# Four summing groups instead of five in layer 0's attention, and a transposed block end in layer 3

## Chip, cores and metric

The kernel runs on one core of a Trainium2 chip. The metric is device time in microseconds (us) from launch to end; lower is better. The core has five engines with queues of their own: TensorE (PE in the profile, with its weight loads as PEld) multiplies matrices into PSUM, VectorE (DVE) and ScalarE (ACT) work elementwise, GpSimd (POOL) does small things here, and SyncE (SP) issues the transfers between HBM and SBUF.

## What is computed

Four layers run one after the other on x of shape (2, 128, 64, 64), each as x = x + layer(group_norm(x)). The change touches the attention of the first and of the last. Cut to these:

```python
# layer 0, per head (4 heads, 32 channels each, n = m = 4096 pixels)
attn1 = softmax(einsum('bhnc,bhmc->bhnm', q1, k1) * temperature, axis=-1)
out1 = einsum('bhnm,bhmc->bhnc', attn1, v)
...
out = conv1x1(out1 + out2, w_po)
...
# layer 3, per head (8 heads, 16 channels each)
a = softmax(einsum('bhcq,bhck->bhqk', q, k) / sqrt(C), axis=-1)
o = einsum('bhqk,bhck->bhcq', a, v)
return o.reshape(B, C, h, w)
```

`out2` is a small attention over channels in layer 0; layers 1 and 2 are convolutions and a product in the Fourier domain. They are left as they are.

## The kernel before

**Softmax in both layers.** No maximum is subtracted (a bound on the exponents is checked at the end, and a general version would run if it were passed). The kernel computes exp(scores), multiplies these weights with the values, and divides the result by the sum of the weights over the keys.

**Layer 0's attention** (`attention` inside `_layer0`, with `_attn_four`). It runs once for each of the two batches. The queries are cut into 8 blocks (`qb`) of 512, the keys into 32 tiles (`kt`) of 128. For each tile of keys, TensorE computes the scores of four heads into two PSUM tiles `ps_s` (L1343; three such tiles exist), ScalarE turns each into `weights` (L1352, 128x1024 each; both halves are one buffer, of which there are four), and TensorE multiplies `vt` with these weights into the accumulator `ps_acc0` (L1760, called by `multiply` one tile behind the scores). PSUM holds the accumulator until the block's last tile; then ScalarE copies it to `used` (L1790).

The sum of the weights takes a second path. VectorE adds the weights of several key tiles elementwise (L1800: `sums`, 128x2048 each, two buffers). How many tiles form such a group says `SUMMED`, by default five groups of 7, 6, 7, 6 and 6 tiles. A group of n tiles takes n - 1 additions: the first tile is only held. When a group is complete, it is put in `pending`, and at the fourth tile of the next group TensorE multiplies it with a block of ones (L1760 again, `sums` and `ones`), which sums over the 128 keys of a tile and accumulates over the groups in `ps_acc1`. After the last group of a block, VectorE transposes that PSUM tile in blocks of 32x32 (`by_query`, L1773), takes the reciprocal of one column in 32 (`rec`, L1775), transposes it back, spread over 32 rows, into `q1` (L1776), and multiplies `used` with it (L1780). `by_query` shares one buffer with the tile `g` of the normalization.

Beside the attention of batch 0 run, woven in one step at every fourth key tile, the channel attention of batch 0 and the normalization of batch 1 (`normalize`: ScalarE makes `g`, TensorE transposes it, VectorE computes statistics and scales, TensorE transposes back). Beside the attention of batch 1 run its channel attention and the statistics of batch 0. Unlike most of the kernel, `attention` isn't inside `_in_order`: the order of its instructions on an engine is that of the tile framework's scheduler. What follows it is in order: batch 1's convolutions after batch 0, and `finish`, the output projection, after batch 1.

**Layer 3's attention** (`attend` inside `_layer3`) is inside `_in_order`. It runs four times (two batches, two halves `t` of the heads), each over 8 blocks of 512 queries and 32 key tiles. Per key tile TensorE computes scores (L2102), ScalarE exponentials (L2112, 128x1024, two per tile), and TensorE multiplies the values two tiles behind (L2121). Here the sums come with the product: the stationary operand holds 16 columns of values and 16 columns of ones for each head, so that in each 32 rows of the accumulator 16 rows are the output and 16 rows the sums, the latter repeated 16 times; which half is which alternates from head to head. There are two accumulators in PSUM; the running block holds one, and the side work that makes the next queries, keys and values uses the other in turn.

At a block's end `done` (L2131) loads the residual of the 64 rows by four DMAs from X, copies the accumulator out of PSUM to `u`, exchanges the halves of each 32 rows into `r` by a stream shuffle, takes the reciprocal of all of `r` (128x512), multiplies, adds the residual, and stores the rows that matter by four DMAs. The 32 block ends are spread over the stage; the last one is the end of the program.

Of the kernel before, what the change touches and what calls it, by code (L numbers as in the profile page):

```python
# [10 lines left out]
F32 = mybir.dt.float32  # L11
# [7 lines left out]
CH = 512  # L19
# [1265 lines left out]


LIMIT = 60.0
SUMMED = (7, 6, 7, 6, 6)
F32R = mybir.dt.float32r
ENGINES = (  # L1290
    mybir.EngineType.PE,
# [117 lines left out]
def _layer0(ctx, tc, X, a, cst, worst, there, dram):  # L1409
# [10 lines left out]
    def acc(n):  # L1420
        return accp.tile([128, CH], F32, tag=f"acc{n}", name=f"ps_acc{n}")
# [330 lines left out]
    def attention(pool, side):  # L1752
        ac = [None, None]
        parts, pending, used = [None], [], {}
        places = [(n, i) for n, size in enumerate(SUMMED) for i in range(size)]

        def four(n, lhs, w, first, last):
            for j in range(4):
                rows = slice(32 * j, 32 * j + 32)
                nc.tensor.matmul(ac[n][rows, :], lhs(rows), w[:, j, :], start=first, stop=last)  # L1760

        def sums():

            while pending:
                qb, n, w = pending.pop(0)
                if n == 0:
                    ac[1] = acc(1)
                four(1, lambda rows: ones, w, n == 0, n == len(SUMMED) - 1)
                if n == len(SUMMED) - 1:

# [11 lines left out]
        def multiply(qb, kt, w):  # L1782
# [13 lines left out]
            else:  # L1796
# [7 lines left out]
                )  # L1804
            if i == SUMMED[n] - 1:
                pending.append((qb, n, parts[0]))
# [156 lines left out]
def _layer3(ctx, tc, X, l3, cst, out, worst, here):  # L1963
    nc = tc.nc
# [4 lines left out]
    two = ctx.enter_context(tc.tile_pool(name="f3_two", bufs=2))  # L1969
# [4 lines left out]
    def acc():  # L1974
        return accp.tile([128, CH], F32, tag="acc", name="ps_acc")
# [118 lines left out]
    def attend(b, t, q, k, vt, early):  # L2094
        ac = [None]

        def scores(qb, kt):
            ps = [spp.tile([128, 2, CH], F32, tag="sp", name="ps_s") for _ in range(2)]
            for n in range(2):
                for j in range(4):  # L2100
                    rows = slice(32 * j, 32 * j + 32)
                    nc.tensor.matmul(  # L2102
                        ps[j // 2][:, j % 2, :],
                        k[rows, kt * 128 : (kt + 1) * 128],
                        q[n][rows, qb * CH : (qb + 1) * CH],
                        start=(n == 0),
                        stop=(n == 1),
                    )
            w = []
            for p in range(2):  # L2110
                w.append(pp.tile([128, 2, CH], F32, tag="weights", name="weights"))
                nc.scalar.activation(w[p], ps[p], AF.Exp)  # L2112
            return w

        def multiply(qb, kt, w):
            if kt == 0:
                ac[0] = acc()
            for j in range(4):

                i = j % 2  # L2120
                nc.tensor.matmul(  # L2121
                    ac[0][32 * j : 32 * j + 32, :],
                    vt[:, kt, j // 2, i : i + 2, :].rearrange("p a d -> p (a d)"),
                    w[j // 2][:, i, :],
                    start=(kt == 0),
                    stop=(kt == NQT - 1),
                )
            if kt == NQT - 1:
                done(qb, ac[0])

        def done(qb, ps):  # L2131
            cols = slice(qb * CH, (qb + 1) * CH)

            places = [
                (slice(32 * j + 16 * (j % 2), 32 * j + 16 * (j % 2) + 16),
                 slice(64 * t + 16 * j, 64 * t + 16 * j + 16))
                for j in range(4)
            ]
            xs = residual[qb % 2]
            for to, rows in places:  # L2140
                nc.sync.dma_start(xs[to, :], X[rows, b, cols])
            u = two.tile([128, CH], F32, tag="u", name="u", bufs=1)
            nc.vector.tensor_copy(u, ps)  # L2143
            r = two.tile([128, CH], F32, tag="r", name="r", bufs=1)
            nc.vector.stream_shuffle(r, u, [(i + 16) % 32 for i in range(32)])  # L2145
            nc.vector.reciprocal(r, r)  # L2146
            nc.vector.tensor_mul(u, u, r)  # L2147
            nc.vector.tensor_add(u, u, xs)  # L2148
            for at, rows in places:
                nc.sync.dma_start(out[b, rows, cols], u[at, :])  # L2150

        waiting = []
        for qb in range(NCH):
            for kt in range(NQT):
                if kt % 2 == 0:
                    over = next(early, early) is early
                waiting.append((qb, kt, scores(qb, kt)))
                if len(waiting) > 2:
                    multiply(*waiting.pop(0))
                yield kt if over else None  # L2160
        for x in waiting:
            multiply(*x)
# [187 lines left out]
```

## Time and profile before

| What | us |
|---|---|
| median of 3 runs | 4205.69 |
| lowest and highest run | 4199.02, 4210.75 |
| the profiled execution's own time | 4197.72 |
| its span, first to last instruction | 4195.9 |
| PE busy | 4026.9 |
| ACT busy | 3332.9 |
| DVE busy | 2127.8 |
| POOL busy | 71.3 |

The profile is of one execution, and its own time stands beside the runs' median: it is one of the shorter ones. Busy shares are means over stages with different limits, so the numbers that matter are those of a stage or of one block, read in the timeline and in windows. Layer 0's two attentions run from about 193 to 806 us and from 1003 to 1596 us, layer 3 from about 2200 us to the end. A line such as `sums<-sums,weights` gives the tile written, then the tiles read; the numbers behind the bar are the busy time of a group in us and the mean of one in ns, and after the second bar stands the idle time ahead of it and what ended it. In the records each fp32 matmul counts twice, so eight records of L1760 are one step of four matmuls.

### The profile page before, as it was taken

The numbers are of one execution on the slowest core, as the hardware profiler recorded it, in microseconds if no ns is written. First come the engines' busy times: TensorE is split into PE (matmuls) and PEld (weight loads), VectorE is DVE, ScalarE is ACT, GpSimd is POOL, SyncE is SP. The second block draws the span as 40 slices with busy tenths as digits, with TensorE's granted clock in tenths as the row PEclk, the third lists the DMA queues.
The fourth block names the chain that finished last, engine by engine and source line by source line (L and its number), as shares of the span: only waits on it lengthen the run. The fifth ranks groups of instructions, "written<-read, shape, count | busy, mean of one in ns | idle before, by whom it ended". The sixth has DMA issues, their size and how long they took to land. (4 is left out here: it accounts for less than half of the span.)

```text
span 4195.9 us, 90633 instructions
## 1 busy us (share of the span) xinstructions
PE 4026.9 (96%) x40014; PEld 1494.0 (36%) x40014; DVE 2127.8 (51%) x2374; ACT 3332.9 (79%) x4035; POOL 71.3 (2%) x145
## 2 busy tenths in 40 slices
PE   7999999989999998997999999999999999999998
PEld 4522222354222224445664333333333333333332
DVE  4678888657888888986754112221132102211111
ACT  4478888735888883326647999999999999999998
POOL 1001000010000001000000000000000000000000
PEclk9999999999999999998999999999999999999999
DMA  1199960000000000004750000000000000000000
GB/s 49 29 188 182 179 90 1 2 2 2 2 1 2 2 1 12 1 1 171 290 208 4 6 6 6 4 6 6 4 6 6 6 4 6 6 4 6 6 6 5
DMA packets 158855, 159.40 MB, mean 38 GB/s; under 512 B 24809, under 2 KB 148713, under 8 KB 154354
## 3 DMA queue, kind: packets, MB, share of 16 engines
q1 hardware_dynamic: 158450, 153.50, 15.7%
q8 instruction: 315, 5.16, 0.5%
q14 instruction: 90, 0.74, 0.1%
HBM read 145.09 MB, written 73.40 MB: 52 GB/s over the span
## 5 line engine op out<-in xcount | busy, mean ns | idle before, releaser
L2112 ACT ACTIVATE weights<-ps_s 128x1024 f32<-128x1024 f32 x2048 | 1884.8, 1099 | 62.8 <-PE ps_s L2102 62.3
L1352 ACT ACTIVATE weights<-ps_s 128x1024 f32<-128x1024 f32 x1024 | 992.9, 1023 | 180.6 <-PE ps_s L1343 164.2
L2121 PE MATMUL ps_acc<-weights,vt 128*32 128x512 f32 x8192 | 1092.8, 605 | 0.0
L2102 PE MATMUL ps_s<-q,k 32*128 32x512 f32 x8192 | 924.9, 444 | 5.4 <-ACT weights L2112 5.4
L1800 DVE TENSOR_TENSOR sums<-sums,weights 128x2048 f32<-128x2048 f32 x352 | 806.7, 2292 | 38.4 <-ACT weights L1352 5.2
L2102 PEld LDWEIGHTS ps_s<-q,k 32*128 32x128 f32 x8192 | 471.2, 182 | 839.4 <-ACT weights L2112 773.6
L1343 PE MATMUL ps_s<-q,k 32*64 32x512 f32 x8192 | 627.3, 613 | 7.1 <-ACT weights L1352 2.4
L1760 PE MATMUL ps_acc<-weights,vt 128*32 128x512 f32 x4096 | 550.9, 606 | 6.6 <-ACT weights L1352 3.6
L2143 DVE COPY u<-ps_acc 128x512 f32<-128x512 f32 x32 | 22.1, 691 | 1039.0 <-PE ps_acc L2121 1039.0
L1343 PEld LDWEIGHTS ps_s<-q,k 32*64 32x64 f32 x8192 | 159.6, 130 | 436.4 <-PE ps_s L1343 320.3
L2121 PEld LDWEIGHTS ps_acc<-weights,vt 128*32 128x32 f32 x8192 | 162.9, 108 | 379.2 <-issue 367.2
L1800 DVE TENSOR_TENSOR sums<-weights 128x2048 f32<-128x2048 f32 x80 | 183.3, 2291 | 113.6 <-ACT weights L1352 113.6
L1760 PEld LDWEIGHTS ps_acc<-weights,vt 128*32 128x32 f32 x4096 | 81.2, 108 | 426.3 <-issue 403.3
L662 DVE SCALAR_TENSOR_TENSOR X<-g,w,X 128x2048 f32<-128x2048 f32 x84 | 197.4, 2350 | 2.6
L1548 PE MATMUL ps_sp<-pad,diag 32*32 32x512 f32 x4608 | 158.9, 597 | 2.3 <-ACT q L1568 1.3
L1008 PE MATMUL ps_z<-w_ri,e 128*32 128x128 f32 x2048 | 137.3, 408 | 14.3 <-DVE e L950 12.1
L2063 DVE TENSOR_TENSOR vt<-ps_acc,bv 128x384 f32<-128x384 f32 x32 | 17.8, 557 | 246.0 <-PE ps_acc L2056 246.0
L1548 PEld LDWEIGHTS ps_sp<-pad,diag 32*32 32x32 f32 x4608 | 95.0, 103 | 54.2 <-issue 15.9
L2033 DVE LOAD_MASK_SELECT qq<-ps_acc x32 | 0.4, 14 | 222.6 <-PE ps_acc L2030 222.6
L2146 DVE RECIPROCAL r<-r 128x512 f32<-128x512 f32 x32 | 107.3, 3353 | 1.1
L950 DVE TENSOR_SCALAR e<-ps_pe 32x136 f32<-32x136 f32 (+1 forms) x352 | 104.4, 297 | 4.9
L948 ACT ACTIVATE e<-ps_pe 32x136 f32<-32x136 f32 (+1 forms) x352 | 99.2, 282 | 4.1
(289 smaller groups left out, 2552.5 us busy)
## 6 DMA issues: line engine op xcount, KB each, us to landing
w_ri<-w_r SPq DMA_DIRECT2D x16, 2112.0 KB, 8.2
w_ri<-w_i SPq DMA_DIRECT2D x16, 2112.0 KB, 13.5
w_r<-in_L_conv_kr_w SPq DMA_DIRECT2D x15, 528.0 KB, 13.5
w_r<-in_L_conv_kr_x SPq DMA_DIRECT2D x15, 528.0 KB, 13.3
w_r<-in_L_conv_kr_y SPq DMA_DIRECT2D x15, 528.0 KB, 13.0
w_r<-in_L_conv_kr_z SPq DMA_DIRECT2D x15, 528.0 KB, 13.2
w_i<-in_L_conv_ki_w SPq DMA_DIRECT2D x15, 528.0 KB, 13.8
w_i<-in_L_conv_ki_x SPq DMA_DIRECT2D x15, 528.0 KB, 12.7
```

The lines of the kernel that those rows point to most:

```text
L662: nc.vector.scalar_tensor_tensor(xi, g[:, i : i + H // 2, j : j + W], w8[:, s : s + 1], xi, ALU.mult, ALU.add)
L950: nc.vector.tensor_scalar_mul(out, got[of, :, s], sign)
L1008: nc.tensor.matmul(out.rearrange("p (n f o) -> p n f o", n=2, f=2), e[:, s, 2 * j : 2 * j + 2, :].rearrange("p f x -> p (f x)"), w.rearran ...
L1343: nc.tensor.matmul(ps[j // 2][to, j % 2, :], k[rows, kt * 128 + 64 * half : kt * 128 + 64 * half + 64], q[rows, qb * CH : (qb + 1) * CH], ...
L1352: nc.scalar.activation(w[:, 2 * p : 2 * p + 2, :], ps[p], AF.Exp)
L1548: nc.tensor.matmul(ps[r // 2][to, r % 2, :].rearrange("p (h w) -> p h w", w=W), diag[rows, grp, t, :], pad[rows, y0 : y0 + ROWS, t % 3 : t ...
L1760: nc.tensor.matmul(ac[n][rows, :], lhs(rows), w[:, j, :], start=first, stop=last)
L1800: nc.vector.tensor_add(parts[0].rearrange("p j c -> p (j c)"), t.rearrange("p j c -> p (j c)"), w.rearrange("p j c -> p (j c)"),)
L2102: nc.tensor.matmul(ps[j // 2][:, j % 2, :], k[rows, kt * 128 : (kt + 1) * 128], q[n][rows, qb * CH : (qb + 1) * CH], start=(n == 0), stop= ...
L2112: nc.scalar.activation(w[p], ps[p], AF.Exp)
L2121: nc.tensor.matmul(ac[0][32 * j : 32 * j + 32, :], vt[:, kt, j // 2, i : i + 2, :].rearrange("p a d -> p (a d)"), w[j // 2][:, i, :], star ...
L2146: nc.vector.reciprocal(r, r)
```

## The change

Two edits. In layer 0 the 32 key tiles of a block form four groups of eight in place of five groups of six or seven: 28 additions on VectorE per block where there were 27, and four matmul groups with `ones` where there were five. In layer 3 the block end is written another way: the accumulator is transposed in blocks of 32x32 straight from PSUM into `z`, so that a query's 16 sums lie along the free axis; the reciprocal is then taken of one column per block of 32, 16 columns in all, for each of the four groups of 32 partitions on its own, since the column alternates; a multiplication with these spread over 32 columns follows, a second transpose brings the result back into `u`, and the addition of the residual and the DMAs stay as they were. The copy, the stream shuffle and the reciprocal over 512 columns are gone. The tile `r` becomes 16 columns wide, with two buffers instead of one, and `z` is new, of 512 columns with one buffer.

```diff
-SUMMED = (7, 6, 7, 6, 6)
+SUMMED = (8, 8, 8, 8)
...
             for to, rows in places:
                 nc.sync.dma_start(xs[to, :], X[rows, b, cols])
+            z = two.tile([128, CH // 32, 32], F32, tag="z", name="z", bufs=1)
+            flat = z.rearrange("p n i -> p (n i)")
+            nc.vector.transpose(flat, ps)
+            r = two.tile([128, CH // 32], F32, tag="r", name="r")
+            for j in range(4):
+                rows = slice(32 * j, 32 * j + 32)
+                nc.vector.reciprocal(r[rows, :], z[rows, :, 16 * (1 - j % 2)])
+            nc.vector.tensor_mul(z, z, r.unsqueeze(2).to_broadcast([128, CH // 32, 32]))
             u = two.tile([128, CH], F32, tag="u", name="u", bufs=1)
-            nc.vector.tensor_copy(u, ps)
-            r = two.tile([128, CH], F32, tag="r", name="r", bufs=1)
-            nc.vector.stream_shuffle(r, u, [(i + 16) % 32 for i in range(32)])
-            nc.vector.reciprocal(r, r)
-            nc.vector.tensor_mul(u, u, r)
+            nc.vector.transpose(u, flat)
             nc.vector.tensor_add(u, u, xs)
             for at, rows in places:
                 nc.sync.dma_start(out[b, rows, cols], u[at, :])
```

## The prediction

> **What bounds the kernel now.** I read the page first, its busy table and its 40 slices, to see which engine fills which stage.
>
> ```profile
> PE   7999999989999998997999999999999999999998
> DVE  4678888657888888986754112221132102211111
> ACT  4478888735888883326647999999999999999998
> ```
>
> Two stages are touched. Layer 0's attention lies in slices 2 to 8 and 10 to 16 (195 to 806 us and 1003 to 1596 us): TensorE is full and VectorE is close behind. Layer 3 is the right half: TensorE and ScalarE are full, VectorE nearly empty. Next, the costliest groups:
>
> ```profile
> L2112 ACT ACTIVATE weights<-ps_s 128x1024 f32<-128x1024 f32 x2048 | 1884.8, 1099 | 62.8 <-PE ps_s L2102 62.3
> ...
> L1800 DVE TENSOR_TENSOR sums<-sums,weights 128x2048 f32<-128x2048 f32 x352 | 806.7, 2292 | 38.4 <-ACT weights L1352 5.2
> L2102 PE MATMUL ps_s<-q,k 32*128 32x512 f32 x8192 | 924.9, 444 | 5.4 <-ACT weights L2112 5.4
> ...
> L2146 DVE RECIPROCAL r<-r 128x512 f32<-128x512 f32 x32 | 107.3, 3353 | 1.1
> ```
>
> L1800 is the addition that layer 0 does once per key tile, except at a group's first: 352 + 80 = 432 = 16 blocks x 27. L2146 is the reciprocal that the change shrinks: large, but on an engine on which layer 3 does not wait. The PE rows of layer 3 lost only 5.4 us waiting.
>
> What matters is one layer 0 block. The window view over a block without side work (from one `used` copy to the next) and over the block with batch 1's normalization beside it:
>
> ```profile
> 588.15:660.64 72.49, 72.24 (x816) 16.15 (x808) 64.00 (x32) 62.47 (x67) 0.00 (x0) 1.00 0.15 18
> 273.54:368.10 94.56, 89.03 (x886) 23.73 (x894) 77.82 (x109) 76.18 (x89) 15.23 (x8) 0.96 1.03 186
> ```
>
> Columns after the stretch: length, then busy PE, PE weight loads, DVE, ACT, POOL. The clean block is TensorE's: 72.24 of 72.49 us. VectorE has 8.5 us over, ScalarE 10. The other block is 22 us longer and nobody is full in it.
>
> The timeline of PE shows the price of one summing matmul group (`ones`), whose starts I subtract:
>
> ```profile
> 652.56 1.28 PE L1343 MATMUL ps_s<-q,k 32*64 32x512 f32 x16
> 653.77 1.07 PE L1760 MATMUL ps_acc<-weights,vt 128*32 128x512 f32 x8
> 654.65 1.04 PE L1760 MATMUL ps_acc<-sums,ones 128*32 128x512 f32 x8
> 655.62 1.11 PE L1343 MATMUL ps_s<-q,k 32*64 32x512 f32 x16
> ...
> 668.46 1.04 PE L1760 MATMUL ps_acc<-sums,ones 128*32 128x512 f32 x8
> ...
> 684.15 1.04 PE L1760 MATMUL ps_acc<-sums,ones 128*32 128x512 f32 x8
> ...
> 697.80 1.04 PE L1760 MATMUL ps_acc<-sums,ones 128*32 128x512 f32 x8
> ```
>
> The timeline of VectorE around the same block end shows its slack:
>
> ```profile
> 672.51 0.71 DVE L1773 STREAM_TRANSPOSE by_query<-ps_acc 128x512 f32<-128x512 f32 x1
> ...
> 679.49 2.28 DVE L1800 TENSOR_TENSOR sums<-weights 128x2048 f32<-128x2048 f32 x1
> 681.88 9.48 DVE L1800 TENSOR_TENSOR sums<-sums,weights 128x2048 f32<-128x2048 f32 x4
> 692.55 2.29 DVE L1800 TENSOR_TENSOR sums<-weights 128x2048 f32<-128x2048 f32 x1 [1.18 <-ACT weights L1352]
> ```
>
> Right after the chain of a block's end a group begins with no idle time; one group later VectorE waits 1.18 us for weights, so it has caught up. Last, the timeline of the end of the program:
>
> ```profile
> 4181.94 0.69 DVE L2143 COPY u<-ps_acc 128x512 f32<-128x512 f32 x1 [50.73 <-PE ps_acc L2121]
> ...
> 4183.50 3.35 DVE L2146 RECIPROCAL r<-r 128x512 f32<-128x512 f32 x1
> ...
> 4187.61 0.69 DVE L2148 TENSOR_TENSOR u<-u,residual 128x512 f32<-128x512 f32 x1
> 4188.33 2.19 SPq L2150 DMA_DIRECT2D out<-u  x4
> ```
>
> Here VectorE is the path: nothing runs beside the last block's end.
>
> **What the Trainium skill says.** "VectorE: DVE Perf Modes", section "The TRN2 errata", gives an fp32 tensor-tensor of N columns as (N+151)/0.96 ns, thus 2291 for 2048; the trace's 2292 agrees[...]. Its section "Two Vector instructions with no wait between them" says that an instruction whose operands start in another quadrant of 32 partitions than those before it starts only when they have finished: that concerns the four reciprocals, and nothing in this trace shows four such in a row.[...]
>
> **Layer 0, clean blocks.** The starts of the summing groups are 654.65, 668.46, 684.15, 697.80 and 713.49. A distance of 6 key tiles is 13.65 us, of 7 tiles 15.69, and 13.81 where the `used` copy falls inside (0.16 more). In order 13.65 + 13.81 + 15.69 + 13.65 + 15.69 = 72.49, the block. The seventh tile costs 2.04; two tiles together cost 4.25 (648.32 to 652.56), so the eighth costs 2.21. A group of eight is then 17.90, and a block 4 x 17.90 + 0.16 = 71.76: 0.73 us less. One group's matmuls start 0.97 us before the next scores, but only some 0.8 to 0.9 of that is lost, since ScalarE's lag is made up meanwhile.
>
> Does VectorE keep up? An addition in a row takes 2.40 us (9.48 for four is 4 x 2.29 and three gaps of 0.10). Before: 27 x 2.40 + 2.65 for the chain transpose, reciprocal, transpose, multiply (672.51 to about 675) = 67.4 of 72.49. After: 28 x 2.40 + 2.65 = 69.9 of 71.76. It stays below, at 97%. What is queued behind a late addition is the release of a `weights` buffer: there are four, and ScalarE's exponentials wait for one. A group's first tile is held until the second's addition ends, so an addition may start about one tile period (2.1 us) late at a group's beginning before ScalarE stalls. At 679.49 it is about 0.5 us late; an eighth tile adds 2.40 - 2.13 = 0.27. So 0.8 of 2.1 is used: no stall, and 1.9 us a block left.
>
> **Layer 0, blocks with side work.** Batch 1's normalization puts about 1.75 us on VectorE every four tiles in the second block and part of the third (346.05 to 347.76). There a group of eight has 7 x 2.40 + 2 x 1.75 = 20.3 us of VectorE work, against 17.9 for TensorE plus its own transposes, 1.6 us a step (L1492 and L1497 are busy 13.0 + 12.8 us over the kernel's 16 steps): 21.1. That is a tie, where groups of six and seven left 0.8 to 1.75 us of idle time each. I take the gain of these two blocks as gone (0), with bounds of -3 (the stalls there shift in our favour) and +4 (one addition in each block, 2.40, less a part). The other 14 blocks give 14 x 0.73 = -10.2.
>
> **Ends of both phases.** The last group has seven additions instead of five to do behind arriving weights; each lags 0.27 more, so the final sum is about 0.55 later. After batch 0 the next convolution's copies waited 4.98 us on that chain (`pad` on `q`, at 810.49), so +0.55. After batch 1 the output projection works from earlier columns meanwhile: 0. Layer 0: -9.7.
>
> **Layer 3.** Per block, 0.69 + 0.72 + 3.35 + 0.69 + 0.69 with gaps = 6.36 us of VectorE (4181.94 to 4188.30) becomes transpose 0.75 (start to next, as at 672.51), four reciprocals of 16 columns at 0.29 each (the layer 0 one takes 0.25 on 128 partitions), multiply 0.73, transpose 0.74, add 0.72: 4.1, with 0.1 for the two small flag operations between. That is 2.1 less; 0.1 off for starts held by quadrant makes 2.0. Bounds: 2.4 if the four overlap, 1.4 if each is held by 0.2. For 31 of 32 blocks this is worth nothing, as TensorE and ScalarE go on beside it; the accumulator is released after 0.71 us instead of 0.69. If that cover were gone, each block would win 2 us, not lose. Only the last block counts: -2.0. The eight DMAs per block are the same.
>
> **Sum.** -9.7 - 2.0 = -11.7 us against the profiled execution's 4197.72 (span 4195.9 and 1.8 around it). The median of the runs is 4205.69, 8 us above this execution; carried over, 4194.0, which is 0.28% less. A measurement of this kernel can tell about 0.3%, 12.6 us, so this forecast lies just within it.
>
> **Rivals.**
> - *The side work takes more.* For it: the second block is already 22 us over a clean one, and the order in layer 0's attention is left to a scheduler (`by_query` at 672.51 ran after an addition that follows it in the program). Against: idle time at each group start there. Loss of 4 more: -7 to -8, about 4198.
> - *Slower: VectorE sets the pace in clean blocks.* Every group starts with a hole until the second tile's weights are there. If the smallest hole of the trace, 1.18 us, remained in each group while the additions run back to back, a block would take 4 x (7 x 2.40 + 1.18) + 2.65 = 74.6, +2.1 each, +33 in all, about 4237 with layer 3's gain. It decides once the holes exceed (72.49 - 69.9) / 4 = 0.65 us. Against: a hole exists only where VectorE has caught up, as at 692.55.
> - *More gain.* If the stalls of the second block (ScalarE waited 3.61 us for the reciprocal in `by_query`'s buffer, TensorE then 3.26) fall away with the new grouping: 6 to 7 more, about 4187.
>
> **How the numbers follow.** Forecast (-8 to -16): 0.62, of which 0.35 is beyond 12.6 us and 0.27 within. Side work: 0.17, within. Slower: 0.15, with 0.14 beyond 0.3%. More gain: 0.06, faster. So faster 0.41, same 0.45, slower 0.14. The range of 4184 to 4208 takes in the forecast with the bounds of side blocks and tail, the side rival and most of the gain rival; the slower rival stays out.
>
> **What would show it.** Clean block of about 71.8 us between `used` copies, four `ones` groups 17.9 apart; VectorE about 66.3 us busy in it (64.00 and one addition); no wait of ScalarE for VectorE there. The second block near 94.6. At the end, about 4.3 us from the last accumulator to the first output DMA. Wrong would be a clean block over 72.5, or gaps of TensorE at block ends in layer 0, or any change in layer 3's 1.83 us per key tile.

## The result and the profile after

| | before | changed |
|---|---|---|
| median of 7 runs each, us | 4209.58 | 4192.23 |
| lowest and highest, us | 4199.02, 4210.75 | 4189.69, 4195.58 |
| profiled execution, its span, us | 4197.72, 4195.9 | 4192.35, 4190.2 |
| mean granted TensorE clock in the profile | 0.985 | 0.983 |

The ratio is 0.9966, with a 95% interval of 0.9955 to 0.9977: 14 us less, 10 to 19 (the ratio pairs runs of the two kernels; the medians alone differ by 17.35 us). The forecast was 11.7 us, or 4194.0.

The two profiles differ by only 5.7 us of span. The profile of before is of an execution of 4197.72 us, below all seven, and its layer 2 had a higher granted clock; this is taken up below. So I compare stretches whose clock is the same, not the spans.

The page of the changed kernel, its row of VectorE in 40 slices and the groups that answer to those shown before:

```profile
DVE  4689999767899998895754102221022102210000
...
L2112 ACT ACTIVATE weights<-ps_s 128x1024 f32<-128x1024 f32 x2048 | 1884.9, 1101 | 61.0 <-PE ps_s L2102 60.6
...
L2102 PE MATMUL ps_s<-q,k 32*128 32x512 f32 x8192 | 924.1, 444 | 5.4 <-ACT weights L2112 5.4
L1800 DVE TENSOR_TENSOR sums<-sums,weights 128x2048 f32<-128x2048 f32 x384 | 880.0, 2292 | 42.6 <-ACT weights L1352 6.4
```

VectorE has more to do in layer 0 (384 + 64 = 448 additions, 16 x 28) and less in layer 3. The large rows of layer 3, L2112 and L2102, are the same to 0.1%.

The window view over two layer 0 blocks of the changed kernel, a clean one and the one with batch 1's normalization beside it (columns as before; the third number from the right is the share of its clock that TensorE was granted):

```profile
584.82:656.61 71.79, 71.48 (x808) 16.05 (x800) 66.28 (x33) 62.46 (x67) 0.00 (x0) 1.00 0.31 26
272.93:366.51 93.58, 87.54 (x878) 23.34 (x886) 80.20 (x107) 76.13 (x88) 13.34 (x8) 0.98 1.07 182
```

The clean block fell from 72.49 to 71.79; the forecast was 71.76. TensorE still fills it, and VectorE went from 64.00 to 66.28 busy, one addition. The timeline of PE shows where the time went, in the starts of the summing groups:

```profile
646.31 1.04 PE L1760 MATMUL ps_acc<-sums,ones 128*32 128x512 f32 x8
...
664.42 1.04 PE L1760 MATMUL ps_acc<-sums,ones 128*32 128x512 f32 x8
...
682.32 1.04 PE L1760 MATMUL ps_acc<-sums,ones 128*32 128x512 f32 x8
...
700.21 1.04 PE L1760 MATMUL ps_acc<-sums,ones 128*32 128x512 f32 x8
```

They are 17.90 apart, 18.11 where the `used` copy lies between. VectorE in the same block:

```profile
668.48 0.71 DVE L1773 STREAM_TRANSPOSE by_query<-ps_acc 128x512 f32<-128x512 f32 x1
...
677.86 2.29 DVE L1800 TENSOR_TENSOR sums<-weights 128x2048 f32<-128x2048 f32 x1
680.25 14.28 DVE L1800 TENSOR_TENSOR sums<-sums,weights 128x2048 f32<-128x2048 f32 x6
694.96 2.29 DVE L1800 TENSOR_TENSOR sums<-weights 128x2048 f32<-128x2048 f32 x1 [0.44 <-ACT weights L1352]
```

The group after the block's end still begins without idle time, and one group later VectorE waits for weights again, 0.44 us where it was 1.18. It has caught up, though by less. ScalarE never waits for `sums` in either attention of the changed kernel.

The end of the program, in the timeline:

```profile
4179.11 0.72 DVE L2144 STREAM_TRANSPOSE z<-ps_acc 128x512 f32<-128x512 f32 x1 [53.09 <-PE ps_acc L2121]
...
4179.92 1.01 DVE L2148 RECIPROCAL r<-z 32x16 f32<-32x16 f32 x4
...
4182.48 0.69 DVE L2152 TENSOR_TENSOR u<-u,residual 128x512 f32<-128x512 f32 x1
4183.20 1.94 SPq L2154 DMA_DIRECT2D out<-u  x4
```

From the accumulator to the first store it takes 4.09 us, where it took 6.39. The four reciprocals take 1.01 together.

Where the time came from, in the two profiles, read from starts of the `used` copies and of the final transposes, each block in us:

```
                            before   changed
batch 0: first block         80.1     78.2    from the first exponential (193.45, 194.75)
         normalization       94.56    93.58   clock 0.96, 0.98
         next                75.07    74.72
         four clean blocks   72.49    71.79   each
         last                71.79    71.02
batch 1: first block         81.97    80.11   from `own` (1001.5, 996.5)
         next, clean         72.50    71.79
         with statistics     74.35    73.66
         last five           361.74   358.48
layer 3: first to last end 1876.5   1874.9
```

The block with the normalization had the better clock in the changed kernel. The kernel that has the old groups and only layer 3's new block end (an experiment below) had a clock of 0.98 there as well:

```profile
274.90:368.67 93.77, 88.24 (x886) 23.74 (x894) 77.80 (x109) 76.10 (x88) 15.23 (x8) 0.98 1.09 194
```

That is 0.2 us more than the changed kernel's 93.58, so of the difference of 1.0 about 0.2 belongs to the change and the rest to the clock.

### The profile page after: what moved, and what is told of

Its sections match the earlier page's. It is cut to its first block, busy times and chain, and to the rows that moved or that the text cites. A ratio compares the mean times of both kernels' runs of the same rounds, so it can differ in the third digit from the quotient of the medians.

```text
span 4190.2 us, 90476 instructions
## 1 busy us (share of the span) xinstructions
PE 4027.6 (96%) x39886; PEld 1505.7 (36%) x39886; DVE 2088.3 (50%) x2454; ACT 3333.8 (80%) x4035; POOL 71.7 (2%) x145
## 5 line engine op out<-in xcount | busy, mean ns | idle before, releaser
L2112 ACT ACTIVATE weights<-ps_s 128x1024 f32<-128x1024 f32 x2048 | 1884.9, 1101 | 61.0 <-PE ps_s L2102 60.6
L2102 PE MATMUL ps_s<-q,k 32*128 32x512 f32 x8192 | 924.1, 444 | 5.4 <-ACT weights L2112 5.4
L1800 DVE TENSOR_TENSOR sums<-sums,weights 128x2048 f32<-128x2048 f32 x384 | 880.0, 2292 | 42.6 <-ACT weights L1352 6.4
L2102 PEld LDWEIGHTS ps_s<-q,k 32*128 32x128 f32 x8192 | 471.2, 182 | 839.7 <-ACT weights L2112 773.1
L2144 DVE STREAM_TRANSPOSE z<-ps_acc 128x512 f32<-128x512 f32 x32 | 22.9, 717 | 1064.6 <-PE ps_acc L2121 1064.6
L1800 DVE TENSOR_TENSOR sums<-weights 128x2048 f32<-128x2048 f32 x64 | 146.6, 2291 | 63.0 <-ACT weights L1352 62.6
L710 PE MATMUL ps_bank<-t,t 128*128 128x512 f32 x224 | 101.3, 610 | 0.0
```

The lines of the kernel that those rows point to most:

```text
L710: nc.tensor.matmul(ps.rearrange("p (h w) -> p h w", w=W), t9[:, k, :], t2[:, c * ROWS + k : (c + 1) * ROWS + k, 2 : W + 2], start=(k == 0) ...
L1800: nc.vector.tensor_add(parts[0].rearrange("p j c -> p (j c)"), t.rearrange("p j c -> p (j c)"), w.rearrange("p j c -> p (j c)"),)
L2102: nc.tensor.matmul(ps[j // 2][:, j % 2, :], k[rows, kt * 128 : (kt + 1) * 128], q[n][rows, qb * CH : (qb + 1) * CH], start=(n == 0), stop= ...
```

## Experiments

Each kernel ran beside the kernel before on the same chip; ratios are to that one. In layer 0 I read block lengths, which repeat to about 0.3 us where the clock is the same, since the whole time scatters by several us.

**The two edits alone.**

```diff
-SUMMED = (7, 6, 7, 6, 6)
+SUMMED = (8, 8, 8, 8)
```

> The groups of eight alone, layer 3's block end as before. Theory (the gain is layer 0's blocks, one summing matmul group less in each): clean blocks of 71.8 us between the `used` copies as against 72.5, layer 0 ends about 12 us earlier relative to the start of its attention, whole kernel 11 to 13 us faster, ratio 0.997. Rival (the gain comes from VectorE's relief in layer 3, 77 us of its work there): ratio 1.000, blocks as they may be.

Ratio 0.9971 (0.9962 to 0.9981), 4197.13 us: 12 us less. Clean blocks of 71.79 us, and all other blocks as in the changed kernel to 0.05. This is the larger part of the gain, and VectorE's relief in layer 3 isn't needed for it.

The other half is the second hunk of the change, with the groups of before:

> The transposed block end alone, groups of 7, 6, 7, 6, 6 as before. Theory: only the last block end counts, so the time from the last accumulator to the first output DMA falls from 6.4 to about 4.1 us and the kernel gains 2 to 3 us (ratio 0.9994, not to be told from 1 by the times); the key-tile period of layer 3 stays at 1.83 us. Rival (VectorE's relief helps TensorE in the stage): ratio 0.998 or less, and fewer us between the first and the last block end of layer 3.

Ratio 0.9986 (0.9978 to 0.9994): 6 us less, with 2.5 to 9 in the interval. More than I expected at its middle, and 1 is outside. The tail measured 4.08 us (4189.53 to 4193.61), as forecast. Going through the 31 distances between block ends one by one, all but a few are those of before to 0.03 us; of these few, three vary by 1.3 to 2.5 us from kernel to kernel with the granted clock (62.25 us at 1.00, 63.54 at 0.97, 64.90 at 0.95). But the tenth, where batch 1's first weights are made, is 61.87 us as against 63.16, both at a clock of 1.00. The timelines there, kernel before:

```profile
2854.01 3.35 DVE L2146 RECIPROCAL r<-r 128x512 f32<-128x512 f32 x1
...
2858.73 0.35 DVE L1996 TENSOR_SCALAR wqk<-w_qk,gn_got 128x256 f32<-128x256 f32 x1
...
2859.14 0.61 PE L2005 MATMUL ps_acc<-gn_got,wqk 128*128 128x1 f32 x4 [1.21 <-DVE wqk L1996]
```

and the changed kernel:

```profile
2851.99 1.02 DVE L2148 RECIPROCAL r<-z 32x16 f32<-32x16 f32 x4
...
2855.13 0.35 DVE L1996 TENSOR_SCALAR wqk<-w_qk,gn_got 128x256 f32<-128x256 f32 x1
...
2856.60 0.61 PE L2005 MATMUL ps_acc<-gn_got,wqk 128*128 128x1 f32 x4
```

`wqk` is queued on VectorE behind the block's end, and a matmul of TensorE behind `wqk`. With the old block end TensorE stood for 1.21 us; with the new one `wqk` is ready in time. So the block end was on the path at two places: the last block and this one. It repeats: the tenth distance is 61.86 to 61.88 us in all ten profiles here of kernels with the new ends throughout, and 63.13 and 63.16 in the two with the old ends and a clock of 1.00.

To see whether any other of the first 31 ends counts, the new end was put into the last block alone:

```diff
+            if b == B - 1 and t == 1 and qb == NCH - 1:
+                z = two.tile([128, CH // 32, 32], F32, tag="r", name="z", bufs=1)
+                flat = z.rearrange("p n i -> p (n i)")
+                nc.vector.transpose(flat, ps)
...
+            else:
+                u = two.tile([128, CH], F32, tag="u", name="u", bufs=1)
+                nc.vector.tensor_copy(u, ps)
...
```

> The new block end in the last of 32 blocks alone, everything else as before. Theory: the last accumulator to the first output DMA takes 4.1 us as in the changed kernel, and the stage from its first to its last block end is as long as before (1876.5 us): the other 31 are worth nothing. Rival: the stage is longer than with all 32 new ends by 1 us or more.

The tail is 4.08 us. The stage is 1880.3 us from the first end to the last, longer than with all 32 new ends by 5.4, so the test as I had set it speaks for the rival. Block by block it doesn't speak for a relief all along the stage: 28 of the 31 distances are those of before. The eighth and the tenth are 2.50 and 1.35 us longer than before, with a granted clock of 0.95 and 0.97 in them, where before had 1.00; the tenth is the block with the wait above. The sum over a stage was the wrong measure. One run, 4206.16 us.

**What sets the pace in layer 0.** Two kernels move one cost each. First, a summing group more on TensorE, with VectorE's additions as they are (the second group of each block counts twice in the sums):

```diff
                 four(1, lambda rows: ones, w, n == 0, n == len(SUMMED) - 1)
+                if n == 1:
+                    four(1, lambda rows: ones, w, False, False)
```

> The changed kernel, but the second group of each block goes through the summing matmuls twice (that group counts double in the sums), so five summing groups on TensorE with still 28 additions on VectorE. Theory (TensorE sets the pace of clean blocks): the clean block returns to 72.6 to 72.8 us from 71.79, 0.8 to 1.0 for the one matmul group. Rival (VectorE sets it): 71.8 stays.

Ratio 0.9995 (0.9986 to 1.0004): layer 0's gain is gone (this kernel still has the new block end of layer 3). A clean block takes 72.65, so this summing group costs 0.86 us. Second, one addition less on VectorE, with four groups (the weights of one key tile are left out of the sums):

```diff
-            else:
+            elif (n, i) != (1, 4):
                 t = parts[0]
```

> The changed kernel with one of the 28 additions of a block left out (the weights of one key tile are missing from the sums), so VectorE's work is that of before and TensorE's that of after. Theory: the clean block stays at 71.8 within 0.1, VectorE's busy time in it falls from 66.3 to 64.0, and the block with the normalization beside it stays within 1 us of 93.6, since VectorE sets the pace in neither. Rival (the additional addition costs something in the side blocks): that block and the next get shorter by 1 to 2.4 us each.

Ratio 0.9973 (0.9957 to 0.9988). The window views of a clean block, first with a group more, then with an addition less:

```profile
588.00:660.60 72.60, 72.30 (x812) 16.33 (x808) 66.23 (x33) 62.40 (x66) 0.00 (x0) 1.00 0.25 24
```

```profile
584.30:656.10 71.80, 71.50 (x808) 16.05 (x800) 64.00 (x32) 62.49 (x66) 0.00 (x0) 1.00 0.30 34
```

VectorE's busy time is 66.23 and 64.00; the length follows TensorE's. With an addition less, the block with the normalization is 93.59 us and the next 74.72, against 93.58 and 74.72 at the same clock: the added addition costs nothing in the side blocks either.

**How far this goes.** More and smaller groups, then fewer and larger:

```diff
+SUMMED = (6, 5, 5, 6, 5, 5)
+SUMMED = (11, 11, 10)
+SUMMED = (16, 16)
```

> Six groups of 6, 5, 5, 6, 5, 5: 26 additions, six summing groups. Theory (price of a summing group read from the distances): 6 tiles take 13.65 and 5 take 13.65 - 2.21 = 11.44, so a clean block of 2 x 13.65 + 4 x 11.44 + 0.16 = 73.2 us, 0.7 more than before and 1.4 more than the changed kernel. Rival (the groups' number matters only by VectorE's additions): 71.8 or less.

A clean block of 73.46, one run of 4211.66 us. The rival (71.8 or less) is refuted; the step from five groups to six is 0.97 us where the theory had 0.7.

> Three groups of 11, 11 and 10: 29 additions, three summing groups. TensorE alone would give about 71.0 us a clean block (0.75 less again), VectorE's back to back 29 x 2.40 + 2.65 = 72.25. Theory: VectorE takes over, clean block 72.3 to 73.5, ScalarE now waits for VectorE, ratio to before 0.997 to 1.003. Rival (VectorE still keeps up): 71.0, ratio 0.994.

Ratio 0.9951 (0.9934 to 0.9967), 4185.57 us. My theory missed: the clean blocks are shorter still, 70.71 at first and 71.09 to 71.38 late in each batch (the interval of the ratio overlaps that of the changed kernel). The window and the timeline of VectorE show what I had wrong:

```profile
512.80:583.50 70.70, 70.40 (x800) 15.63 (x792) 68.00 (x34) 62.45 (x67) 0.00 (x0) 1.00 1.00 158
```

```profile
515.63 2.29 DVE L1800 TENSOR_TENSOR sums<-weights 128x2048 f32<-128x2048 f32 x1
518.02 7.08 DVE L1800 TENSOR_TENSOR sums<-sums,weights 128x2048 f32<-128x2048 f32 x3
525.02 0.71 DVE L1773 STREAM_TRANSPOSE by_query<-ps_acc 128x512 f32<-128x512 f32 x1
...
586.73 2.29 DVE L1800 TENSOR_TENSOR sums<-weights 128x2048 f32<-128x2048 f32 x1
```

From one block's first addition to the next, 515.63 to 586.73, VectorE never idles: 29 additions and the block's end take 71.10 us, not 72.25. The transpose starts at 525.02, before the recorded end of the three additions ahead of it (525.10). The profile of before had the same starts, and I had read them wrongly:

```profile
670.30 2.29 DVE L1800 TENSOR_TENSOR sums<-sums,weights 128x2048 f32<-128x2048 f32 x1
...
674.29 0.69 DVE L1780 TENSOR_TENSOR q<-used,q 128x512 f32<-128x512 f32 x1
674.90 4.68 DVE L1800 TENSOR_TENSOR sums<-sums,weights 128x2048 f32<-128x2048 f32 x2
```

An addition that reads the `sums` of the one ahead starts 2.40 after it. An instruction that doesn't read the result of an addition ahead starts 2.21 after it (the transpose at 672.51 after 670.30, a new group at 679.49). The block's end takes 2.39, from 672.51 to 674.90, not 2.65. With these numbers 28 additions in four groups come to 23 x 2.40 + 5 x 2.21 + 2.39 = 68.6 us, 29 in three groups to 25 x 2.40 + 4 x 2.21 + 2.39 = 71.2, 30 in two to 73.8. TensorE sets 71.79 with four groups and 70.71 with three. So with three groups VectorE falls behind by 0.4 us a block, the buffers take that up for some blocks, and then ScalarE begins to wait (1.1 us in all between 441 and 800 us). Two places outside the clean blocks lose with three groups: each batch's first block (80.7 us, against 78.2 in batch 0 of the changed kernel) and the stretch between the batches (200.2 against 197.1, at the same clock of 0.97).

> Two groups of 16: 30 additions, two summing groups. TensorE alone would give about 69.9 us; VectorE back to back, as read with 29 additions (2.37 each and 2.4 for the block's end), 30 x 2.37 + 2.4 = 73.5. Theory: clean block 73.3 to 74.5 with ScalarE waiting for VectorE in every block: the point where VectorE takes over lies between 28 and 30 additions. Rival (VectorE still hides): 70 to 71.

Clean blocks of 73.69 to 74.04 in batch 0, near the 73.8 of the sum above; 4225.43 us in one run. The waits of that kernel between 440 and 790 us (who waits for whom, us in total, times, longest):

```profile
ACT weights L1352 <- DVE sums L1800: 32.0, 70, 0.7
```

Here VectorE has taken over: the slower rival of the prediction exists, but at 30 additions, not at 28.

**The stall in the block with the normalization.**

```diff
-by_query = cp.tile([128, CH // 32, 32], F32, tag="g", name="by_query", bufs=1)
+by_query = pool.tile([128, CH // 32, 32], F32, tag="by_query", name="by_query", bufs=1)
```

> The changed kernel with a buffer of its own for `by_query`, which no longer shares one with the normalization's `g`. Theory (the second block's 22 us over a clean one hold a stall by this buffer: ScalarE waits 3.6 us for the reciprocal, TensorE then 3.3): that wait goes, the second block falls from 93.6 to about 90, kernel 3 us faster than the changed one, ratio to before 0.996. Rival (the wait only uncovers VectorE, which is late there anyway): the second block stays within 1 us of 93.6.

Ratio 0.9948 (0.9935 to 0.9962). The second `g` of ScalarE in that block, in the changed kernel and in this one:

```profile
294.86 0.81 ACT L1486 ACTIVATE g<-X,gn_shift,gn_got 128x512 f32<-128x512 f32 x1 [3.61 <-DVE rec L1775]
```

```profile
287.83 0.84 ACT L1486 ACTIVATE g<-X,gn_shift,gn_got 128x512 f32<-128x512 f32 x1
```

It comes 7 us earlier and waits for nothing. TensorE's wait of 3.3 us behind it is gone as well, and the block takes 90.81 us instead of 93.58, though at a lower granted clock. That is about 3 us, but they don't reach the end of the attention in this profile. The window view of the block, and of the stretch from batch 0's last `used` copy to `own` of batch 1 in the changed kernel and in this one:

```profile
272.29:363.10 90.81, 89.00 (x878) 23.86 (x886) 77.93 (x106) 76.08 (x89) 17.15 (x8) 0.96 1.18 201
```

```profile
799.42:996.50 197.08, 170.86 (x2758) 106.37 (x2766) 108.30 (x173) 75.31 (x129) 13.53 (x40) 0.97 0.01 2
```

```profile
796.01:997.10 201.09, 175.85 (x2758) 109.03 (x2766) 108.27 (x172) 75.32 (x129) 13.52 (x40) 0.95 0.01 2
```

The stretch takes 4.0 us more at a lower clock, and from the first exponential to the last `used` copy it is 1386.7 us against 1385.8. The shorter whole of this profile lies between layer 0's last `used` copy and layer 3's first block end (711.7 us against 723.7), almost all of it work that this edit doesn't touch. So the wait is removed, but what that is worth for the kernel isn't shown, and the intervals of the two ratios overlap.

**The changed kernel again, and all gains together.** The unaltered changed kernel ran beside a version with three groups, the buffer, and the last four stores issued by SyncE and ScalarE in turn.

> The changed kernel once more, unaltered, beside the others on the same chip. Theory (the difference of the two first profiles, 5.4 us, is smaller than that of the medians because TensorE's granted clock in layer 2 and the convolutions differs from one execution to the next): the ratio to before lies again between 0.9955 and 0.9977, block lengths in layer 0 repeat to 0.3 us, and what differs from the first profile sits where the granted clock differs. Rival (layer 2 is made slower by the change): layer 2 is again 8 to 11 us longer than in the profile of before, with the clock alike.

Ratio 0.9965 (0.9951 to 0.9979). Clean blocks repeat to 0.01 us; the block with the normalization does not (96.24, with a granted clock of 0.95, against 93.58 with 0.98), so my 0.3 us holds only for blocks at an equal clock. Layer 2's main stretch and the one after it, in the window view of before and of the first profile of the changed kernel, and the second of them in this one:

```profile
1954.80:2188.50 233.70, 210.23 (x2552) 139.76 (x2552) 164.36 (x447) 135.22 (x408) 0.00 (x0) 0.93 0.65 260
2188.50:2197.90 9.40, 7.27 (x59) 6.61 (x60) 1.42 (x10) 3.65 (x8) 0.00 (x0) 1.00 0.01 2
```

```profile
1942.80:2180.20 237.40, 213.62 (x2552) 142.13 (x2552) 164.44 (x447) 135.45 (x408) 0.00 (x0) 0.91 0.65 256
2180.20:2194.30 14.10, 12.27 (x58) 11.47 (x59) 1.39 (x10) 3.75 (x8) 0.00 (x0) 0.56 0.01 1
```

```profile
2182.80:2192.10 9.30, 7.18 (x59) 6.52 (x60) 1.37 (x9) 3.66 (x8) 0.00 (x0) 1.00 0.01 2
```

The stretch of 9.40 us took 14.10 at 0.56, and 9.30 again at 1.00. From 1954.80 to the last addition of layer 2, before took 266.4 us, the first profile 277.2, this one 269.9. So layer 2 isn't made slower by the change by the 8 to 11 us of the rival; the first pair of profiles had one execution with a better clock and one with a worse. The main stretch, 233.7 in before and 237.4 in the changed kernel, goes both ways with either grouping: the kernel with the new block end alone, with the old groups, has 237.1, the one with the buffer of its own, with the new groups, 233.7.

> Three groups (11, 11, 10), a buffer of its own for `by_query`, and the last four stores issued from two queues, on top of the changed kernel. Theory (the gains add): 6 us from the groups, 3 from the second block's stall, 1 from the stores, so about 10 us less than the changed kernel, ratio to before 0.994; clean blocks 70.7 to 71.4. Rival (VectorE is at its limit with 29 additions, and the stall's removal only shifts its lateness): no more than the three groups alone, ratio 0.995 or above.

Ratio 0.9937 (0.9924 to 0.9951), 4183.21 us: about 10 us less than the changed kernel beside it (4193.44), as forecast. The block with the normalization takes 89.80, but at a clock of 1.00 where the kernel with three groups alone had 93.37 at 0.96, so how much of this is the buffer isn't told. Clean blocks take 70.71 to 71.12, and the last stores are issued in 0.86 us instead of 1.94 and 2.17 in the two profiles of the changed kernel. The interval overlaps those of the three groups alone and of the buffer alone, so that all three gains add isn't shown.

## Why the prediction was right, step by step

- *Clean blocks.* Right, mechanism and size: 0.73 forecast, 0.70 measured, VectorE's busy time as forecast. The two shifted kernels show that TensorE alone sets the length.
- *VectorE keeps up.* Right, with more room than stated. The block's end was taken as 2.65 us where it is 2.39, and every addition as 2.40 where, with no waits, five in a block take 2.21: about 68.6 us for 28 additions, not 69.9. That is 96% of the block, not 97%.
- *Blocks with side work.* "I take the gain of these two blocks as gone (0)" was near: 0.2 us at an equal clock in the first, 0.36 in the second. The reason given was not: leaving an addition out changes nothing in them, so the tie of 20.3 against 21.1 us did not set their length. ScalarE and TensorE stand waiting in the first of them, and the buffer experiment removed one of these waits.
- *First blocks.* The term mis-sized: counted at 0.73 each, they gained about 1.9. The scores that stood 1.16 us for `a2t` in each batch before (at 244.81) stand 0.26 (at 245.36), because a summing group now starts inside that wait, at 244.07; a wait of 0.4 for `w` is gone too. That is luck of where the groups fall: with three groups the same scores stand 2.0 us, and the first block of batch 0 takes 80.7 us.
- *Ends of both phases.* The sign was right, the size was not: ScalarE's `pad` copies waited 4.98 us on the chain after batch 0 and wait 5.13, so 0.15 and not 0.55. The whole stretch (196.6 and 197.1 us) can't show it; with the old groups it took 196.6 to 197.9.
- *Layer 3.* The last end: 2.3 us measured against 2.0. "For 31 of 32 blocks this is worth nothing" failed for one: the tenth gained 1.3 us, because I looked for waits on the block end in sums over the stage and not at what is queued behind it when a new batch's weights are made.
- *Sum.* At an equal clock layer 0 gained about 12 us where 9.7 was the term, layer 3 3.6 where 2.0 was. That is 16, near the 14 of the measured ratio and inside its interval. The total was near because the clean blocks, the largest term, were right; the larger errors, the first blocks and the tenth end, both left gain out. The prediction gave its largest single chance (0.45) to a change within 0.3%; the measured 0.34% lies just above that, with the interval on both sides of it.
- *Rivals.* More loss by side work: refuted by the kernel with an addition less. Slower by VectorE: refuted at 28 additions, and its assumption too, that a hole of 1.18 us stays in each group: with 29 additions no hole is left, since a late engine finds its inputs waiting. More gain by a stall that vanishes: it did not vanish with the change. It can be removed, which shortens its block by about 3 us; a gain of the whole kernel from it isn't shown.

## What to carry to other kernels

Where one engine fills a repeated block, price an edit by the distance between the starts of equal instructions on that engine. Here that forecast 0.73 us for the group removed, and 0.70 came; but the price depends on how the groups divide the tiles: 0.86 for a group added to four, 0.97 from five to six, 1.08 from four to three. For a second engine that is nearly as full, sum the distances from start to start as well, those at a change of instruction included, and not one rate for all: read so, the profile of before gives 68.6, 71.2 and 73.8 us for 28, 29 and 30 additions, and so places the point where VectorE takes over. And work off the critical path is on it wherever something on that engine is queued behind it: look at each place where the stage changes its input, not at the steady state alone. Before a difference between two profiles is credited to an edit, compare the granted clock of the stretch.

## What the runs showed that was not expected

- The granted TensorE clock differs from one execution to the next at the same place: 1.00, 0.56 and 1.00 in three profiles of layer 2's last stretch, worth 4.7 us there. From layer 0's last `used` copy to layer 3's first block end, almost all of it work that no edit here touches, the 13 profiles took 711.7 us (clock 0.94) to 723.7 (clock 0.92), so single profiles of two kernels can differ by 10 us without an edit's doing.
- VectorE takes 0.24 us for a reciprocal of 32 partitions by 16 columns, and four in a row in different groups of partitions take 1.01 together: each starts 0.01 us after the one ahead ends. The Trainium skill (VectorE: DVE Perf Modes, Two Vector instructions with no wait between them) says that an instruction in another group of partitions is held until the earlier ones have finished; the run agrees with it. The prediction had 1.16 us for the four, and 0.1 more for starts held so.
